# The tail of a sandwich kernel: residual added from the PSUM banks, and down products placed chunk by chunk between the steps of the routing

## The chip, the cores and the metric

The kernel runs on one core of a Trainium2 chip. The metric is the device time of one execution in microseconds. The engines are named as the profile names them: PE (matmuls, with PEld for its weight loads), DVE, ACT, POOL and SP, which only issues transfers here.

## The reference

The input x has 8 sequences of 512 rows and 256 columns, all in float32. Two blocks follow each other, each with a layernorm before and one after it:

```python
x = x + _layernorm(_L0_attn_ref(_layernorm(x), wq, bq, wkv, bkv, wo))
x = x + _layernorm(_L0_ffn_ref(_layernorm(x), gate_w, w_gate, w_up, w_down, sh_gate, sh_up, sh_down))

def _layernorm(x, axis=-1, eps=1e-05):
    m, v = mean(x), var(x)                    # over the 256 columns
    return (x - m) / sqrt(v + eps)
```

The attention has 16 heads of 128 columns in 4 groups of keys and values, is causal, and adds position codes to queries and keys. The feed-forward part has a shared expert of 352 hidden columns, `(silu(x @ sh_gate.T) * (x @ sh_up.T)) @ sh_down.T`, and 64 routed experts of 176 hidden columns. Each row chooses its 6 best experts by a softmax over 64 logits; each expert takes at most 64 rows, in the order of the rows over all 8 sequences, and the chosen outputs are added with their softmax weights.

## The kernel before

A sequence's 512 rows lie as 4 blocks of 128 (`NI`), so most tiles are 128 partitions by 4 blocks by 256 columns. The main loop runs over 128 pairs of sequence and head. In one step of it the scores of head k, the mixing of head k-2 and the output projection of head k-3 are issued. The projections of a sequence add up over its 16 heads in two PSUM banks, `po`. The feed-forward work of sequence b-1 is cut into small steps and put at fixed places of the loop over sequence b. The order of every engine's instructions is written out by hand (a manual schedule): each engine works through its own list in program order, and semaphores are placed where a tile or a bank is handed on.

The routed experts are done in two parts. The rows of sequences 0 to 4 are gathered from DRAM for all 32 pairs of experts and added back into DRAM. For sequences 5 to 7 one pair of experts ("late") still has free places; each of these sequences marks the rows for it (`marks`), gathers them by a matmul (`gather`, tile `ptx_late`), computes the pair (`gate_up`, `gate_up_hidden`, `turn_hidden`, `down`, tiles `pgu_late`, `hid_late`, `pth_late`, `ht_late`, `pd_late`, `dd_late`), and adds the result by a matmul with the turned marks `gt`. (A loop behind everything serves further pairs with free places; in the traced execution it has no round to run.) The last outputs of the early sequences come from `finish_early`, a generator whose steps read two partial sums (L661), take their statistics, scale them on ACT (L97), add x on POOL (L649) and store (L651). Sequence 4 is the last of these.

`last_part` (its head is `def last_part(before, spare)`) runs behind the last head. It has this to do: the end of sequence 6's shared expert (`shared6`), its routed result and output (`output6`); the whole feed-forward part of sequence 7; and the rest of `finish_early` (`spare`). The names that the text uses:

- `st_o`, `mv_o`, `ve_o`, `rs_o`, `shift_o`: statistics of sequence 7's attention output, taken from the banks `po`; mean and variance, variance plus epsilon, its power -1/2 (on POOL), and minus mean times that. The same with `_f` for the layernorm before the feed-forward part, and with `_y` for the one after it.
- L821 and L822: x plus the scaled attention output `o`, and the statistics of the sum. `scale_on_act` (L97) makes `o` on ACT.
- `xg`, `pt_f`, `xt2` (shown as `o_xt` by the profile, which shares its tile with `o`): the normalized rows, their transposes, and the copies of these.
- `psg`, `psu`, `gs`, `hid`: gate and up products of the shared expert for one chunk of hidden columns. There are three chunks, taken in the order 2, 1, 0. Chunk 2 is 96 wide and carries the 64 router logits in the partitions behind it; these are copied to `lg`. After the tanh (`gs`, ACT), two DVE operations (L692, L693) finish `hid` for a chunk.
- `pg`, `most`, `sc`, `top`, `left`, `chosen`, `pp`, `places`: the steps of the choices in `route`: turned logits, their maximum, exponentials (L388), the best eight, the marked choices, a running count by matmul, and each row's place with its expert.
- `py`: the down products of the shared expert (L698) together with the routed result (`dd_late` by `gt`: L714 for sequence 6, L859 for sequence 7), in two PSUM banks.

For sequence 6, chunk 2 of `hid` is ready before the last head; chunks 1 and 0 are left to `last_part`. PSUM banks come from three pools: `ps_s` (three banks, tag s), `ps_m` (three, tag m) and `ps_o` (two). A bank is given again in turn, so a matmul into it waits until the last reader of three allocations ago is done.

Of the kernel before, what the change touches and what calls it, by code (L numbers as in the profile page):

```python
# [44 lines left out]
def sandwich_kernel(ctx, tc, x, wq, bq_t, wkv, bk_t, bv, wo, gate_wt, w_gate, w_up, w_down,  # L45
# [50 lines left out]
    def scale_on_act(dst, src, rs, shift, i):  # L96
        nc.scalar.activation(dst, src, AF.Identity, bias=shift[:, i : i + 1], scale=rs[:, i : i + 1])  # L97
# [25 lines left out]
    with ExitStack() as part:  # L123
# [545 lines left out]
        def shared(b, xt2, l, banks="mmmmmm"):  # L669

            hid = p1.tile([P, len(SH_CHUNKS), T], F32, tag="hid", name=f"hid_{b}")
            banks = iter(banks)

            for n, (f0, fw) in reversed(list(enumerate(SH_CHUNKS))):
                mw = min(P, fw + NX // 2)
                pgu = []
                for w_sb, name in ((sg_sb, "psg"), (su_sb, "psu")):
                    tag = next(banks)
                    pp = {"m": ps_m, "s": ps_s}[tag].tile([P, T], F32, tag=tag, name=f"{name}_{b}_{n}")
                    for c in range(NC):  # L680
                        nc.tensor.matmul(pp[:mw, :], lhsT=w_sb[:, c, ds(f0, mw)], rhs=xt2[:, c, :],
                                         start=c == 0, stop=c == NC - 1)
                    pgu.append(pp)
                if fw < P:
                    l["lg"] = p1.tile([NX, T], F32, tag="y", name=f"lg_{b}")
                    on_act(l["lg"][: NX // 2, :], pgu[0][fw:, :])
                    on_act(l["lg"][NX // 2 :, :], pgu[1][fw:, :])

                gs = p2.tile([P, T], F32, tag="gs", name=f"gs_{b}_{n}", bufs=1)
                nc.scalar.activation(gs[:fw, :], pgu[0][:fw, :], AF.Tanh, scale=0.5)  # L690
                yield
                nc.vector.scalar_tensor_tensor(gs[:fw, :], gs[:fw, :], 1.0, pgu[0][:fw, :], ALU.add, ALU.mult)  # L692
                nc.vector.scalar_tensor_tensor(hid[:fw, n, :], gs[:fw, :], 0.5, pgu[1][:fw, :], ALU.mult, ALU.mult)  # L693
                yield
# [6 lines left out]
            if b == B - 1:  # L701
                l["py"] = [ps_o.tile([P, 2, E], F32, tag=f"o{n}", name=f"py_{b}_{n}") for n in range(2)]
                for i in range(NI):
                    products(i, l["py"][i // 2][:, i % 2, :], i % 2 == 0, False)
                yield
                return
# [14 lines left out]
        def feed_forward(b):  # L721
# [41 lines left out]
            def go(which, n=1):  # L763
                return lambda: [next(l[which]) for _ in range(n)]
# [36 lines left out]

            steps["shared"], steps["output"] = go("f"), lambda: next(l["out"]) if "out" in l else begin_output()
            return steps

        def last_part(before, spare):
# [4 lines left out]
            shared6, output6 = before["shared"], before["output"]  # L810
            shared6()
            mv, rs = norm_scales([sums[i // 2][:, i % 2, :] for i in range(NI)], f"o{b}")
            shared6()
            shared6()
            shift = shifts(mv, rs, f"o{b}")
            two = p2.tile([P, 2, NI * E], F32, tag="v", name="o_xt2")
            o, xt2 = two[:, 0].rearrange("p (i e) -> p i e", i=NI), two[:, 1].rearrange("p (c t) -> p c t", c=NC)
            st = small.tile([P, NI, 6], F32, tag="st", name=f"st_f{b}")
            for i in range(NI):
                scale_on_act(o[:, i, :], sums[i // 2][:, i % 2, :], rs, shift, i)  # L820
                nc.vector.tensor_add(xt[:, i, :], xt[:, i, :], o[:, i, :])  # L821
                nc.vector.bn_stats(st[:, i, :], xt[:, i, :])  # L822
            mv, rs = scales_of(st, NI, f"f{b}")
            shared6()
            shift = shifts(mv, rs, f"f{b}")
            nc.sync.dma_start(out=rows_of(x1_d, b * T), in_=xt)
            xg = p1.tile([P, NI, ROW], F32, tag="xg", name=f"xg_{b}")
            for i in range(NI):
                if i % 2:
                    scale_on_act(xg[:, i, :E], xt[:, i, :], rs, shift, i)  # L830
# [12 lines left out]
            next(r)  # L843
# [17 lines left out]
            shared6()  # L861
            output6()
            output6()
# [188 lines left out]
```

## Time and profile before

| what | value |
|---|---|
| median of 3 runs | 1479.51 us (1479.34 to 1482.35) |
| the profiled execution's own time | 1482.25 us |
| its span, first to last instruction | 1480.5 us |
| mean granted PE clock | 0.986 |
| busy PE, DVE, ACT, POOL | 1404.6, 887.2, 507.5, 424.8 us |
| last matmul of the last head's projection starts / `pd_late` of sequence 7 starts | 1412.30 / 1460.17 us |
| last sum (L872) ends / last store is issued | 1468.8 / 1469.33 us |

Times of single instructions count from the start of the span. A busy share says how long an engine had an instruction under way; it says nothing on whether the next one waited. For that one reads the idle time that a row gives in brackets, with what ended it. The last 70 us of the span belong to `last_part` and the wait for its stores; nothing that the change edits runs earlier.

### The profile page before, as it was taken

How to read it: one execution, taken by the hardware profiler on the slowest of the kernel's cores; microseconds unless marked ns; L12 is line 12 of the kernel's file. 1: busy time of each engine (PE TensorE's matmuls, PEld its weight loads, DVE VectorE, ACT ScalarE, POOL GpSimd, SP SyncE). 2: the span in 40 equal slices, each digit the busy share in tenths (PEclk: the TensorE clock that was granted, in tenths of full speed). 3: DMA queues.
4: the chain of work that ended last, by engine and by line, in shares of the span. 5: the costliest groups of instructions: out<-in, count | busy, mean ns of one | idle time of the engine just before them, and what ended most of it. 6: DMA issues, size and time to landing. Idle time of an engine off the chain costs nothing. (4 is left out here: it accounts for less than half of the span.)

```text
span 1480.5 us, 18545 instructions
## 1 busy us (share of the span) xinstructions
PE 1404.6 (95%) x5310; PEld 853.3 (58%) x5310; DVE 887.2 (60%) x3094; ACT 507.5 (34%) x1450; POOL 424.8 (29%) x682
## 2 busy tenths in 40 slices
PE   9999999999999999999999999989899999899985
PEld 5656655666565655665566555655455655455553
DVE  5555576657655666557665766666455554567543
ACT  2333333233422333233323333233233243344432
POOL 2222231123211321123112411234434343523311
PEclk9999999999999999999999999999999999999998
DMA  7664554355444554445435554459999889668711
GB/s 257 195 181 142 156 169 144 105 158 163 150 132 131 160 153 137 121 152 168 142 107 157 162 151 136 132 184 252 253 236 242 240 232 255 179 194 259 211 47 62
DMA packets 160790, 252.03 MB, mean 170 GB/s; under 512 B 16412, under 2 KB 136189, under 8 KB 160685
## 3 DMA queue, kind: packets, MB, share of 16 engines
q1 hardware_dynamic: 131149, 206.76, 46.4%
q10 hardware_dynamic: 23392, 34.61, 8.6%
q0 software_dynamic: 6144, 9.44, 3.4%
q8 instruction: 44, 0.72, 0.2%
q14 instruction: 61, 0.50, 0.1%
HBM read 143.01 MB, written 107.74 MB: 169 GB/s over the span
## 5 line engine op out<-in xcount | busy, mean ns | idle before, releaser
L306 POOL TENSOR_SCALAR e<-e,recip 128x128 f32<-128x128 f32 x508 | 266.2, 557 | 802.6 <-DVE recip L303 775.1
L296 ACT ACTIVATE e<-e,least 128x128 f32<-128x128 f32 (+3 forms) x512 | 285.6, 559 | 388.9 <-DVE least L293 346.0
L289 PE MATMUL psc<-kt,qt 128*128 128x128 f32 (+3 forms) x1024 | 311.2, 441 | 24.3 <-DVE least L293 12.1
L349 PE MATMUL pav<-et,v 128*128 128x512 f32 (+3 forms) x1024 | 297.2, 433 | 5.3 <-ACT dd L584 5.3
L349 PEld LDWEIGHTS pav<-et,v 128*128 128x128 f32 x1024 | 194.0, 190 | 168.4 <-issue 117.9
L293 DVE CUSTOM_DVE_ANT_0 e<-psc,mask 128x128 f32<-128x128 f32 (+3 forms) x512 | 231.4, 478 | 52.1 <-PE psc L289 46.6
L361 PE MATMUL po<-wo_sb,ao 128*128 128x256 f32 x1024 | 243.5, 381 | 0.7 <-ACT ao L109 0.7
L276 PE MATMUL pq<-xnt,wq_sb 128*128 128x512 f32 x512 | 241.7, 594 | 1.0 <-ACT sc L388 0.7
L361 PEld LDWEIGHTS po<-wo_sb,ao 128*128 128x128 f32 x1024 | 192.5, 190 | 68.7 <-issue 37.4
L322 DVE STREAM_TRANSPOSE eb<-e 128x128 f32<-128x128 f32 x756 | 227.3, 364 | 4.0 <-DMA ex_d<-eb 4.0
L289 PEld LDWEIGHTS psc<-kt,qt 128*128 128x128 f32 x1024 | 166.0, 191 | 106.4 <-DVE least L293 37.7
L109 ACT COPY ao<-pav 128x512 f32<-128x512 f32 x128 | 75.0, 586 | 436.4 <-PE pav L349 416.5
L279 DVE SCALAR_TENSOR_TENSOR qt<-pq,bq_sb,pe_sb 128x512 f32<-128x512 f32 x128 | 95.7, 748 | 110.1 <-PE pq L276 110.1
L276 PEld LDWEIGHTS pq<-xnt,wq_sb 128*128 128x128 f32 x512 | 96.3, 191 | 71.9 <-issue 64.3
L303 DVE RECIPROCAL recip<-total 128x4 f32<-128x4 f32 x128 | 22.8, 178 | 126.8 <-ACT e L296 126.8
L296 ACT ACTIVATION_READ_ACCUMULATOR e<-e,least 128x1 f32 x512 | 95.7, 187 | 0.0
L585 POOL DMA_INDIRECT y_d<-dd,idx x32 | 50.9, 1591 | 113.4 <-DMA y_d<-dd,idx 80.3
L248 PE MATMUL pk<-xnt,wkv_sb 128*128 128x512 f32 x128 | 60.4, 594 | 0.2 <-ACT xnt L109 0.2
L259 PE MATMUL pv<-wkv_sb,xnt 128*128 128x512 f32 x128 | 60.2, 593 | 0.0
L261 DVE TENSOR_TENSOR v<-pv,bv_sb 128x512 f32<-128x512 f32 x32 | 22.1, 691 | 61.8 <-PE pv L259 61.8
L251 DVE SCALAR_TENSOR_TENSOR kt<-pk,bk_sb,pe_sb 128x512 f32<-128x512 f32 x32 | 24.0, 750 | 48.9 <-PE pk L248 48.9
L112 DVE COPY ht<-pth 88x256 f32<-88x256 f32 x32 | 13.4, 418 | 63.5 <-PE pth L566 63.4
(193 smaller groups left out, 1121.5 us busy)
## 6 DMA issues: line engine op xcount, KB each, us to landing
ex_d<-eb SPq DMA_DIRECT2D x126, 640.0 KB
et<-ex_d SPq DMA_DIRECT2D x504, 160.0 KB
wgu<-in_w_gate ACTq DMA_DIRECT2D x32, 352.0 KB
wgu<-in_w_up ACTq DMA_DIRECT2D x32, 352.0 KB
wd<-in_w_down ACTq DMA_DIRECT2D x32, 352.0 KB
y<-y_d SPq DMA_DIRECT2D x10, 512.0 KB
x<-in_x SPq DMA_DIRECT2D x8, 512.0 KB
x_d<-x SPq DMA_DIRECT2D x8, 512.0 KB
```

The costliest lines, as they stand in the source:

```text
L109: nc.scalar.copy(dst, src)
L248: nc.tensor.matmul(pk, lhsT=wkv_sb[:, c, g, 0, :], rhs=s["xnt"][:, c, :], start=c == 0, stop=c == NC - 1)
L259: nc.tensor.matmul(pv, lhsT=s["xnt"][:, c, ts(i, P)], rhs=wkv_sb[:, c, :, 1, :], start=c == 0, stop=c == NC - 1)
L276: nc.tensor.matmul(pq, lhsT=wq_sb[h // QPG][:, c, ts(h % QPG, D)], rhs=seqs[b]["xnt"][:, c, :], start=c == 0, stop=c == NC - 1)
L279: nc.vector.scalar_tensor_tensor(qt, pq, bq_sb[:, h : h + 1], pe_sb, ALU.add, ALU.add)
L289: nc.tensor.matmul(psc[:, :w], lhsT=l["qt"][:, ts(i, P)], rhs=seqs[b]["kt"][h // QPG][:, :w], start=True, stop=True)
L293: nc.vector.tensor_tensor_reduce(out=e, in0=psc[:, :w], in1=mask[:, T - w :], scale=-1.0 / math.sqrt(D), scalar=BIG, op0=ALU.add, op1=ALU. ...
L296: nc.scalar.activation(e, e, AF.Exp, bias=l["least"][:, i : i + 1], scale=-1.0, accum_out=l["total"][:, i : i + 1])
L306: engine.tensor_scalar(e, e, recip[:, n : n + 1], 1.0, ALU.mult, ALU.mult)
L322: nc.vector.transpose(blocks.rearrange("p c j t -> p j c t"), l["e"][i][:, js[0] * P : (js[-1] + 1) * P].rearrange("p (j c t) -> p j c t", ...
L349: nc.tensor.matmul(pav[:, :, j:, :], lhsT=seqs[b]["v"][:, j, ts(g, D)], rhs=l["et"][:, :, AT[j] : AT[j] + NI - j, :], start=j == 0, stop=j ...
L361: nc.tensor.matmul(po[b][i // 2][:, i % 2, :], lhsT=ao[:, ts(i, P)], rhs=wo_sb[:, h, :], start=h == 0 and i % 2 == 0, stop=h == NH - 1, sk ...
```

## The change

`shared` no longer finishes everything in one order. For sequences 6 and 7 it hands out three pieces, and `last_part` places them: `hidden(n)` is the pair of DVE operations for chunk n of sequence 6, `part(py, n)` is the four down products of chunk n, and `late(py)` the four products of the routed result with the copies to `y` and the store. Chunk 0 of sequence 6 takes its `gs` from another pool tag (`qt`), so that two of them can be held.

In `last_part` the residual is added with one DVE operation from the bank, x + po * rs (L843 of the changed kernel). The shift that is left out there is added on POOL later (L861), since the layernorm that follows takes a row's mean off anyway. In the output the same is done with two DVE operations: subtract the mean from the bank (L901), then multiply and add (L903). Sequence 4's scaling and sums come first in `last_part`, its store comes last of all, and sequence 6's output is issued ahead of sequence 7's final products.

The order that this gives on each engine (sequence in brackets where it matters):

- PE: psg_1, psu_1, psg_0, psu_0 (6); chunk 2 of py (6); transposes pt_f; chunk 0; psg_2, psu_2 (7); chunk 1; pg; routed products (6); psg_1, psu_1 (7); pp; psg_0, psu_0 (7); gather; turned marks; pgu; chunks 2 and 1 (7); pth; chunk 0; pd; routed products (7).
- DVE: shift_y (4); statistics of po; four times L843 and statistics; shift_o; mv_f, ve_f; hidden(0); shift_f; two blocks of xg; hidden(1); copy of pt_f_1; the choices up to chosen; hidden of chunk 2 (7); places, marks; hidden of chunk 1 (7); copy gxt; hidden of chunk 0 (7); hid_late; copy ht; statistics of y (6); statistics of py (7); four L901; four L903.
- ACT: y scaling (4); tanh of chunks 1 and 0 (6); two blocks of xg; and from there as before without the scalings that DVE took over.
- POOL: x_4's four sums, rs_o, rs_f, four times L861, rs_y (6), x_6's four sums, rs_y (7).
- SP: x1 store, y_6 store, xg store, places store, output of 6, y_7 store, two halves of the output of 7, output of 4.

```diff
+            def part(py, n):
+                fw = SH_CHUNKS[n][1]
+                for i in range(NI):
+                    nc.tensor.matmul(py[i // 2][:, i % 2, :], lhsT=hid[:fw, n, ts(i, P)], rhs=sd_sb[:fw, n, :],
+                                     start=n == 2 and i % 2 == 0, stop=False, skip_group_check=True)
+
+            def late(py):
+                l["y"] = p1.tile([P, NI, E], F32, tag="y", name=f"y_{b}")
+                for i in range(NI):
+                    nc.tensor.matmul(py[i // 2][:, i % 2, :], lhsT=l["gt"][:, ts(i, P)], rhs=l["dd"], start=False,
+                                     stop=True, skip_group_check=True)
+                    if i % 2:
+                        on_act(l["y"][:, i - 1 : i + 1, :], py[i // 2])
+                nc.sync.dma_start(out=rows_of(ly_d, b * T - ET_ROWS), in_=l["y"])
...
-                gs = p2.tile([P, T], F32, tag="gs", name=f"gs_{b}_{n}", bufs=1)
+                gs = (p2.tile([P, T], F32, tag="qt", name=f"gs_{b}_{n}") if b == B - 2 and n == 0 else
+                      p2.tile([P, T], F32, tag="gs", name=f"gs_{b}_{n}", bufs=1))
                 nc.scalar.activation(gs[:fw, :], pgu[0][:fw, :], AF.Tanh, scale=0.5)
+
+                def hidden(n=n, fw=fw, gs=gs, pgu=pgu):
+                    nc.vector.scalar_tensor_tensor(gs[:fw, :], gs[:fw, :], 1.0, pgu[0][:fw, :], ALU.add, ALU.mult)
+                    nc.vector.scalar_tensor_tensor(hid[:fw, n, :], gs[:fw, :], 0.5, pgu[1][:fw, :], ALU.mult, ALU.mult)
...
         def last_part(before, spare):
...
-            shared6, output6 = before["shared"], before["output"]
+            other, shared6, output6 = before["l"], before["shared"], before["output"]
+            next(spare, None)
             shared6()
             mv, rs = norm_scales([sums[i // 2][:, i % 2, :] for i in range(NI)], f"o{b}")
-            shared6()
-            shared6()
-            shift = shifts(mv, rs, f"o{b}")
+            next(other["f"])
...
-            for i in range(NI):
-                scale_on_act(o[:, i, :], sums[i // 2][:, i % 2, :], rs, shift, i)
-                nc.vector.tensor_add(xt[:, i, :], xt[:, i, :], o[:, i, :])
+            for i in range(NI):
+                nc.vector.scalar_tensor_tensor(xt[:, i, :], sums[i // 2][:, i % 2, :], rs[:, i : i + 1], xt[:, i, :],
+                                               ALU.mult, ALU.add)
                 nc.vector.bn_stats(st[:, i, :], xt[:, i, :])
+            shift = shifts(mv, rs, f"o{b}")
+            py6 = [ps_o.tile([P, 2, E], F32, tag=f"o{n}", name=f"py_{b - 1}_{n}") for n in range(2)]
+            other["part"](py6, 2)
             mv, rs = scales_of(st, NI, f"f{b}")
-            shared6()
-            shift = shifts(mv, rs, f"f{b}")
-            nc.sync.dma_start(out=rows_of(x1_d, b * T), in_=xt)
+            other["hidden"](0)
+            fshift = shifts(mv, rs, f"f{b}")
...
+            other["hidden"](1)
             transpose_rows(xt2, xg, f"f{b}")
+            for i in range(NI):
+                nc.gpsimd.tensor_scalar(xt[:, i, :], xt[:, i, :], shift[:, i : i + 1], 1.0, ALU.add, ALU.mult)
+            nc.sync.dma_start(out=rows_of(x1_d, b * T), in_=xt)
+            other["part"](py6, 0)
             f = shared(b, xt2, l, "msmsms")
             next(f)
+            other["part"](py6, 1)
             r = route(b, xg, l)
-            for _ in spare:
-                pass
             next(r)
-            shared6()
+            other["late"](py6)
             next(r)
             next(r)
+            next(f)
+            next(f)
             next(r)
             marked = marks(table["m"], xg[:, :, E:ROW], table["places"], b, p2, "xnt")
             next(f)
             next(f)
             gather("late", [(xg, marked[0])])
             gt = turn_scores(marked[1], b, p2, "kt", 5)
-            next(f)
             gate_up("late")
             next(f)
+            py = l["py"] = [ps_o.tile([P, 2, E], F32, tag=f"o{n}", name=f"py_{b}_{n}") for n in range(2)]
+            l["part"](py, 2)
+            l["part"](py, 1)
             gate_up_hidden("late")
-            next(f)
             turn_hidden("late")
-            next(f)
+            l["part"](py, 0)
             down("late")
-            py = l["py"]
+            output6()
+            output6()
+            output6()
             for i in range(NI):
                 nc.tensor.matmul(py[i // 2][:, i % 2, :], lhsT=gt[:, ts(i, P)], rhs=pairs["late"]["dd"],
                                  start=False, stop=True, skip_group_check=True)
-            shared6()
-            output6()
-            output6()
...
-            shift = shifts(mv, rs, f"y{b}")
-            for i in range(NI):
-                scale_on_act(o[:, i, :], py[i // 2][:, i % 2, :], rs, shift, i)
-                nc.vector.tensor_add(xt[:, i, :], xt[:, i, :], o[:, i, :])
+            for i in range(NI):
+                nc.vector.tensor_scalar(o[:, i, :], py[i // 2][:, i % 2, :], mv[:, i, 0:1], None, ALU.subtract)
+            for i in range(NI):
+                nc.vector.scalar_tensor_tensor(xt[:, i, :], o[:, i, :], rs[:, i : i + 1], xt[:, i, :],
+                                               ALU.mult, ALU.add)
                 if i % 2:
                     nc.sync.dma_start(out=rows_of(out, b * T)[:, i - 1 : i + 1, :], in_=xt[:, i - 1 : i + 1, :])
-            output6()
+            for _ in spare:
+                pass
```

More of the change, by code (lines that the diff above doesn't have):

```diff
@@ L671, in shared @@
             hid = p1.tile([P, len(SH_CHUNKS), T], F32, tag="hid", name=f"hid_{b}")
-            banks = iter(banks)
+            banks, todo = iter(banks), {}
+            def part(py, n):
[11 more added lines that the diff above has]
+                nc.sync.dma_start(out=rows_of(ly_d, b * T - ET_ROWS), in_=l["y"])
+            l |= {"late": late, "part": part, "hidden": lambda n: todo.pop(n)()}
             for n, (f0, fw) in reversed(list(enumerate(SH_CHUNKS))):
@@ L687, in shared @@
                     on_act(l["lg"][NX // 2 :, :], pgu[1][fw:, :])
-                gs = p2.tile([P, T], F32, tag="gs", name=f"gs_{b}_{n}", bufs=1)
+                gs = (p2.tile([P, T], F32, tag="qt", name=f"gs_{b}_{n}") if b == B - 2 and n == 0 else
+                      p2.tile([P, T], F32, tag="gs", name=f"gs_{b}_{n}", bufs=1))
                 nc.scalar.activation(gs[:fw, :], pgu[0][:fw, :], AF.Tanh, scale=0.5)
+                def hidden(n=n, fw=fw, gs=gs, pgu=pgu):
+                    nc.vector.scalar_tensor_tensor(gs[:fw, :], gs[:fw, :], 1.0, pgu[0][:fw, :], ALU.add, ALU.mult)
+                    nc.vector.scalar_tensor_tensor(hid[:fw, n, :], gs[:fw, :], 0.5, pgu[1][:fw, :], ALU.mult, ALU.mult)
+                todo[n] = hidden
                 yield
-                nc.vector.scalar_tensor_tensor(gs[:fw, :], gs[:fw, :], 1.0, pgu[0][:fw, :], ALU.add, ALU.mult)
-                nc.vector.scalar_tensor_tensor(hid[:fw, n, :], gs[:fw, :], 0.5, pgu[1][:fw, :], ALU.mult, ALU.mult)
-                yield
+                if b != B - 2 or n == 2:
+                    todo.pop(n)()
+                    yield
+            if b >= B - 2:
+                return
             def products(i, py, first, last):
@@ L699, in products @@
                                      stop=last and n == len(SH_CHUNKS) - 1, skip_group_check=True)
-            if b == B - 1:
-                l["py"] = [ps_o.tile([P, 2, E], F32, tag=f"o{n}", name=f"py_{b}_{n}") for n in range(2)]
-                for i in range(NI):
-                    products(i, l["py"][i // 2][:, i % 2, :], i % 2 == 0, False)
-                yield
-                return
             y = l["y"] = p1.tile([P, NI, E], F32, tag="y", name=f"y_{b}")
@@ L800, in feed_forward @@
                                 "14B": go("out"), "15A": go("out")}
+            steps["l"] = l
             steps["shared"], steps["output"] = go("f"), lambda: next(l["out"]) if "out" in l else begin_output()
@@ L829, in last_part @@
                 if i % 2:
-                    scale_on_act(xg[:, i, :E], xt[:, i, :], rs, shift, i)
+                    scale_on_act(xg[:, i, :E], xt[:, i, :], rs, fshift, i)
                 else:
                     normalize(xg[:, i, :E], xt[:, i, :], mv, rs, i)
+            other["hidden"](1)
             transpose_rows(xt2, xg, f"f{b}")
+            for i in range(NI):
+                nc.gpsimd.tensor_scalar(xt[:, i, :], xt[:, i, :], shift[:, i : i + 1], 1.0, ALU.add, ALU.mult)
+            nc.sync.dma_start(out=rows_of(x1_d, b * T), in_=xt)
+            other["part"](py6, 0)
             f = shared(b, xt2, l, "msmsms")
             next(f)
+            other["part"](py6, 1)
             r = route(b, xg, l)
-            for _ in spare:
-                pass
             next(r)
-            shared6()
+            other["late"](py6)
             next(r)
             next(r)
+            next(f)
+            next(f)
             next(r)
```

## The prediction

> **What bounds the kernel now.** I read the page first, then the table of windows over the last 80 us, then the order of time from 1405 us on, then the groups by form for single durations. The page says that TensorE has work to the very end (its chain of waits names only the last residual sum, L872):
>
> ```profile
> PE 1404.6 (95%) x5310; PEld 853.3 (58%) x5310; DVE 887.2 (60%) x3094; ACT 507.5 (34%) x1450; POOL 424.8 (29%) x682
> ...
> PEclk9999999999999999999999999999999999999998
> ```
>
> The 95% is an average over 128 heads. The change touches only what comes after the last head, so its own stretch decides. In the windows (columns: PE, PEld, DVE, ACT, POOL busy us, granted clock, DMA share, GB/s) one row stands out:
>
> ```profile
> 1410.00:1420.00 10.00, 9.27 (x29) 5.24 (x28) 3.42 (x12) 1.70 (x4) 1.01 (x1) 1.00 0.00 0
> 1420.00:1430.00 10.00, 4.94 (x14) 2.48 (x13) 6.31 (x20) 3.58 (x8) 1.01 (x1) 0.78 0.16 55
> 1430.00:1440.00 10.00, 9.33 (x34) 6.07 (x33) 1.94 (x9) 5.47 (x16) 2.77 (x4) 0.88 0.05 16
> 1440.00:1450.00 10.00, 9.65 (x61) 6.47 (x59) 6.72 (x23) 1.77 (x3) 0.00 (x0) 1.00 0.50 167
> ```
>
> From 1421 us PE is idle for 5 us, and afterwards its clock is low. The order of time shows the chain (start, duration, engine, line, what; idle time before it and what ended that):
>
> ```profile
> 1415.66 1.01 POOL L87 TENSOR_TENSOR rs_o<-ve_o,mhalf 128x4 f32<-128x4 f32 x1 [10.58 <-DVE ve_o L85]
> ...
> 1419.97 1.93 ACT L97 ACTIVATE o_xt<-po,shift_o,rs_o 128x256 f32<-128x256 f32 x4
> ...
> 1420.57 0.43 DVE L821 TENSOR_TENSOR x<-x,o_xt 128x256 f32<-128x256 f32 x1 [2.04 <-ACT o_xt L97]
> ...
> 1426.22 2.04 PE L119 MATMUL pt_f<-ident,xg 128*128 128x128 f32 x8 [5.06 <-DVE xg L106]
> ...
> 1428.08 3.78 PE L681 MATMUL psg<-o_xt,sg_sb 128*128 128x512 f32 x4
> ...
> 1435.08 2.06 ACT L97 ACTIVATE y<-y,shift_y,rs_y 128x256 f32<-128x256 f32 x4
> ...
> 1437.05 0.30 ACT L388 ACTIVATE sc<-pg,most 128x64 f32<-128x64 f32 x1
> ...
> 1460.17 1.08 PE L575 MATMUL pd_late<-wd_late,ht_late 88*64 88x256 f32 x8
> ```
>
> The reader is to see three losses. rs_o is ready at 1416.67, but the first sum starts at 1420.57, because shift_o (1418.37) stands behind two shared-expert operations on DVE and the scaling behind a tanh on ACT. PE then waits 5.06 us, and psg takes 3.78 us where the same four matmuls take 1.88 at 1414.13. And the exponentials of the choices (L388), wanted from 1435.54 on, wait for the y scaling of an early sequence until 1437.05. From the gate transposes (1434.62) to pd (1460.17) PE is nearly full: there the order of work sets the end.
>
> **The change part by part.** All PE work is kept: 24 products py by hid, 8 by gt. PE durations at full clock, from starts in the order of time: a pair psg and psu 3.44 us (1414.13 to 1417.56), one chunk of four products 1.72 (1436.85 to 1438.15 is six passes in 1.30, a chunk is eight).
>
> 1. *x_4 moved forward.* shift, scaling and sums of sequence 4 go to the start. ACT scales right after its ao copy (end 1412.25); from first scaling to last sum took 1435.08 to 1438.57, 3.49 us, so POOL is done at 1415.75, and only then takes rs_o, which is behind it in POOL's queue. The row says nothing worse than 0.1 us against 1415.66. But ve_o (1415.41) now falls beside a POOL sum:
>
> ```profile
> L85 DVE TENSOR_SCALAR ve_o<-mv_o 128x4 f32<-128x4 f32 x8 | 3.8, 470 | 0.3
> ...
> L85 DVE TENSOR_SCALAR ve_f<-mv_f 128x4 f32<-128x4 f32 x8 | 1.4, 178 | 0.3
> ```
>
>    The same operation averages 470 ns where POOL works beside it and 178 where it does not. The Trainium skill, page "SBUF — State Buffer", section "Who interferes with whom", says why: VectorE in a two-port mode and GpSimd lock one another out for a whole instruction. By the row ve_o ends 0.3 us late on average; by the rule it waits for the running sum, to 1415.75, and ends at 1415.95. I take the rule's: rs_o 1416.0 to 1417.05. The sum by the row alone would be 0.1 us better.
> 2. *Residual straight from the banks.* No scaling on ACT, no o. Four L843 (scale, add, 128x256 from PSUM) alternate with the statistics. No such operation is in the trace; the nearest is L418 (PSUM plus SBUF, 128x256, mean 410 ns) against L821, which it replaces, 412: the four pairs keep 3.24 us (1420.57 to 1423.81). Bounds: 0 and +0.4 us (0.1 each). So 1417.1 to 1420.35, then shift_o 0.15, and 1.86 as before (1423.81 to 1425.67) to xg: 1422.4, 3.3 earlier. hidden(0) lies in that stretch now as then, beside POOL's rs_f; its tanh ends at 1420.08 as before, psu at 1421.16, neither late.
> 3. *Chunk 2 before the transposes.* It fills PE from 1421.0 to 1422.7. xg's last row block comes 1.21 after the first (1425.67 to 1426.88), at 1423.6, the transposes end at 1424.3. PE idles in crumbs only, so the clock stays full.
> 4. *hidden(1), then pt_f_1's copy on DVE*: 0.73 of xg, 1.5 of hidden, 0.69 of copy: done at 1425.4. The cover is chunk 0 on PE, 1424.3 to 1426.0; without it the wait would be 0.4. psg_2 starts at 1426.0 (before 1428.08). The four POOL sums of shift_o and x1's store move behind xg; nobody waits for them before the last sum. POOL's first may hold the second xg by one operation (502 ns by L306's form), but ACT's fourth block is later anyway: 0 to 0.3, I take 0.
> 5. *Chunk 1 before pg.* psg_2, psu_2 3.44, chunk 1 1.72: pg at 1431.2 (before 1434.62). Its input lg would be there at 1430.3, so this chunk costs 0.9 here and pays later.
> 6. *Choices.* pg to most 0.50, most 0.42, and no scaling ahead on ACT: sc at 1432.15 instead of 1437.05. To chosen's end 4.64 as before (1437.05 to 1441.69): 1436.8. Meanwhile PE does pg 0.46, the gt products 1.72, psg_1 and psu_1 3.44: to 1436.8. ly_d's store goes ahead of lxg_d's on SP, its input is older. y_6's copies on ACT follow the exponentials, as before.
> 7. *hidden(2) between chosen and places* on DVE: 1.5 us on the way to the marks (places 1438.3, before 1442.65; marks for the gather 1.82 later, 1440.1). PE does pp (0.55) and, once hidden(2)'s first half has freed the bank at 1437.55, psg_0 and psu_0, to 1441.05. So the gather starts on PE's account, at 1441.1 (before 1446.41), and hidden(2) costs 0.2.
> 8. *To pd.* Gather to pgu 2.56, pgu 1.33, both as before: 1445.0. Chunks 2 and 1: 3.44; the late hidden (ready 1446.2) is covered by them. pth 0.4, chunk 0 1.72 covering the ht copy: pd at 1450.55, 9.6 before 1460.17.
> 9. *The end.* py from dd, statistics, ve: 4.67 after pd's start as before, 1455.2. y_6's scale is ready only 3.15 after ht's copy (1455.06 to 1458.2 before), at 1452.4, so its POOL sums run to 1455.9 and, by the lock of part 1, hold ve to 1456.05 (0 to 0.7). Then rs 1.05 beside four L901; L901 is new, taken at L418's 0.43 each, 1.7, then four L903 at L872's 0.43: 1459.55, against 1468.83: 9.3 earlier. ACT's copies of y_7 end by 1455.9 and hold nothing.
> 10. *Stores.* x_4's 0.5 MB leaves last, at 1460.05, where x_6's left at 1469.33 before; x_6's goes at 1455.9. Four half-megabyte stores instead of three fall into the end: at the 338 GB/s of 1470 to 1472 they need 6.2 us from about 1456.8: 1463.0; before, the last landed near 1472.2. 9.2 earlier.
>
> Sum: 9.2 us. Of the 9.6 to pd, 3.4 come by pg, 1.5 more by sc, and the rest because sequence 6's hid products now fill PE's early wait and the four psg and psu products of chunks 1 and 0 the wait for the choices, instead of standing behind both. Unknown costs (items 1, 2, 4, 9) lie within -0.5 and +1.2. Against its own time (span 1480.5, time 1482.25, 1.75 outside the span) that is a span of 1471.3 and a time of 1473.0; the median of the runs, 1479.51, is 2.74 below the profiled time, so I expect 1479.5 - 9.2 = 1470.3, rounded up to 1470.5 for small waits not seen.
>
> **The rivals.**
> - *The clock falls all the same.* A wait of 5.06 us preceded the low clock here, and 3.43 us at 1385 (psc 3.91 us for eight, 2.42 otherwise); 1.22 us at 1364 did not. If chunk 2 comes late, psg_2 and psu_2 again cost 2.2 more: 7.0 us gain, 1472.5. Against: chunk 2 needs the banks read by 1420.0, one us before PE asks.
> - *PE's order gives part back.* Chunks ahead of pg, pth and pd hold critical work whenever a producer is early, and DVE's new hiddens hold places. If three such places cost 1 to 1.5 us each, the gain is 5 to 6: 1474. For: item 5 shows one of 0.9.
> - *Slower: the clock stays low.* The Trainium skill, page "TensorE: Matmul & The Clock Gate", section "A second HAM failure mode: psum-queue depth-cycling", has a kernel whose short PE waits between groups made the clock swing. Here the new part is full of such crumbs (0.2 before the transposes, at pp, at pgu). After 1421 some 31 us of PE work lie on the path, each at half clock costs as much again; slower than before from 9.2 us of that work at half clock, with all of it some 22 us slower (1501). By the row, 0: the stretch 1400 to 1420 has waits of 0.73 us and less, and a clock of 1.00. I take the row.
> - *No effect* would need another end than this part; the last things in the trace are this part's own sums and stores, so it gets next to nothing.
>
> **How the numbers follow.** My forecast 0.80 (1468.5 to 1472), the clock rival 0.07, PE's order 0.08, no effect 0.02, slower 0.03. The range, 1468.0 to 1474.5, takes in the first three but for the outer tenth. A measurement of this kernel can tell 0.2%, 3 us, from no change; the first three all exceed that, a fraction of the third aside: faster 0.94, same 0.03, slower 0.03.
>
> **What would show it.** Right: no PE wait over 1 us after the last po; clock 1.00 in 1420 to 1440; psg_2 in 1.9 us; L843 near 1417; sc near 1432; pd near 1450.5; last store near 1460. Wrong: ve_o or rs_o later than 1417.5, L843 above 0.55 us, a granted clock below 0.95 there, pd after 1453, or stores landing more than 3.5 us after the last issue.

## The result, and the profile after

Eight runs of the changed kernel have a median of 1469.33 us (1466.1 to 1477.28); eight of the kernel before, 1480.72 (1471.45 to 1484.6). The ratio is 0.9944, with a 95% interval of 0.992 to 0.9968: a gain of 8.3 us, between 4.7 and 11.8. (The ratio is not the quotient of the two medians, which lie 11.4 us apart; that too is inside the interval.) The forecast was 1470.5.

The profiled execution of after has a span of 1469.4 us, a time of 1471.22 and a mean clock of 0.992. Of the page:

```profile
PE 1398.0 (95%) x5310; PEld 851.9 (58%) x5310; DVE 887.6 (60%) x3097; ACT 503.8 (34%) x1442; POOL 428.9 (29%) x686
...
PEclk9999999999999999999999999999999999999998
```

The number of matmuls is the same, and their busy time is 6.6 us less, part of it time at a low clock that is gone. The share still says 95%, as before; this view would have shown nothing. The windows of after (columns as in the prediction) do:

```profile
1410.00:1420.00 10.00, 9.43 (x28) 5.31 (x29) 6.71 (x25) 3.69 (x7) 4.65 (x6) 1.00 0.01 2
1420.00:1430.00 10.00, 9.95 (x43) 6.62 (x42) 3.36 (x8) 3.43 (x6) 2.10 (x5) 1.00 0.15 53
1430.00:1440.00 10.00, 9.90 (x46) 5.58 (x45) 8.15 (x30) 2.86 (x11) 0.00 (x0) 1.00 0.38 131
1440.00:1450.00 10.00, 9.66 (x57) 7.04 (x55) 4.57 (x16) 1.71 (x4) 0.60 (x1) 1.00 0.01 2
```

From 1420 to 1430 PE was busy for 4.94 us at a clock of 0.78; it is busy for 9.95 us at 1.00. In the order of time of after:

```profile
1411.10 2.79 POOL L649 TENSOR_TENSOR x<-x,y 128x256 f32<-128x256 f32 x4 [7.90 <-ACT y L97]
...
1413.68 0.23 DVE L85 TENSOR_SCALAR ve_o<-mv_o 128x4 f32<-128x4 f32 x1
1413.99 1.02 POOL L87 TENSOR_TENSOR rs_o<-ve_o,mhalf 128x4 f32<-128x4 f32 x1
...
1415.04 0.48 DVE L843 SCALAR_TENSOR_TENSOR x<-po,rs_o,x 128x256 f32<-128x256 f32 x1 [1.13 <-POOL rs_o L87]
...
1421.01 1.48 PE L119 MATMUL pt_f<-ident,xg 128*128 128x128 f32 x8
...
1424.05 1.88 PE L699 MATMUL psg<-o_xt,sg_sb 128*128 128x512 f32 x4
...
1430.25 0.31 ACT L388 ACTIVATE sc<-pg,most 128x64 f32<-128x64 f32 x1 [1.38 <-DVE most L384]
...
1448.66 1.08 PE L575 MATMUL pd_late<-wd_late,ht_late 88*64 88x256 f32 x8
...
1453.33 0.17 DVE L85 TENSOR_SCALAR ve_y<-mv_y 128x4 f32<-128x4 f32 x1
1453.41 1.65 DVE L901 TENSOR_SCALAR o_xt<-py,mv_y 128x256 f32<-128x256 f32 x4
1454.11 1.02 POOL L87 TENSOR_TENSOR rs_y<-ve_y,mhalf 128x4 f32<-128x4 f32 x1
...
1455.16 1.67 DVE L903 SCALAR_TENSOR_TENSOR x<-o_xt,rs_y,x 128x256 f32<-128x256 f32 x4
```

pt_f follows the py products with no wait in its bracket, where before there were 5.06 us, and takes 1.48 us instead of 2.04; psg takes 1.88 instead of 3.78.

One care in reading these times. The main loop, which nobody edited, does not take the same time in two executions: the last head's projection (the last L361 on PE) starts at 1412.30 us in the trace of before, at 1410.57 in that of after, and between 1407.30 and 1417.08 in the experiments' traces. So everything below is counted from that start, the mark. What is left between two kernels is then their tail alone. The whole-run ratio, which has the loop's scatter in it, is given beside it.

| from the start of the last projection, us | before | after | difference | predicted |
|---|---|---|---|---|
| first sum of the residual starts | 8.27 | 4.47 | -3.80 | 4.8 |
| transposes pt_f start | 13.92 | 10.44 | -3.48 | about 10.5 |
| psg_2 starts | 15.78 | 13.48 | -2.30 | 13.7 |
| pg starts | 22.32 | 18.73 | -3.59 | 18.9 |
| sc starts | 24.75 | 19.68 | -5.07 | 19.85 |
| pd_late starts | 47.87 | 38.09 | -9.78 | 38.25 |
| last sum of the output ends | 56.53 | 46.26 | -10.27 | 47.25 |
| span ends | 68.20 | 58.83 | -9.37 | 59.0 |

The predicted column is the prediction's time less 1412.30. The two profiled spans differ by 11.1 us; 9.4 of them are the tail, the other 1.7 are the loop's scatter.

How PE spent the time from the mark to pd_late, before and after (columns as in the prediction):

```profile
1412.30:1460.17 47.87, 41.23 (x160) 25.53 (x160) 22.92 (x78) 12.85 (x30) 5.80 (x7) 0.93 0.15 50
1410.57:1448.66 38.09, 37.85 (x160) 24.07 (x161) 22.24 (x71) 10.90 (x26) 6.75 (x10) 1.00 0.15 49
```

The same 160 matmuls lie in both stretches. Of the 9.78 us between them, 6.40 are idle time of PE that is gone (6.64 before, 0.24 after), and 3.38 are matmuls that take less time, most of it the low clock (2.3 us by e1_fill below). Up to pd_late the new kernel has nothing left to fill.

### The profile page after: what moved, and what is told of

It reads as the page before. It is cut to its first block, busy times and chain, and to the rows that moved or that the text cites. A ratio compares the mean times of both kernels' runs of the same rounds, so it can differ in the third digit from the quotient of the medians.

```text
span 1469.4 us, 18542 instructions
## 1 busy us (share of the span) xinstructions
PE 1398.0 (95%) x5310; PEld 851.9 (58%) x5310; DVE 887.6 (60%) x3097; ACT 503.8 (34%) x1442; POOL 428.9 (29%) x686
## 5 line engine op out<-in xcount | busy, mean ns | idle before, releaser
L289 PE MATMUL psc<-kt,qt 128*128 128x128 f32 (+3 forms) x1024 | 310.6, 441 | 23.1 <-DVE least L293 11.2
L361 PE MATMUL po<-wo_sb,ao 128*128 128x256 f32 x1024 | 243.5, 381 | 0.7 <-ACT ao L109 0.7
L361 PEld LDWEIGHTS po<-wo_sb,ao 128*128 128x128 f32 x1024 | 192.6, 190 | 69.0 <-issue 37.6
L279 DVE SCALAR_TENSOR_TENSOR qt<-pq,bq_sb,pe_sb 128x512 f32<-128x512 f32 x128 | 95.8, 748 | 111.2 <-PE pq L276 111.1
```

The lines of the kernel that those rows point to most:

```text
L279: nc.vector.scalar_tensor_tensor(qt, pq, bq_sb[:, h : h + 1], pe_sb, ALU.add, ALU.add)
L289: nc.tensor.matmul(psc[:, :w], lhsT=l["qt"][:, ts(i, P)], rhs=seqs[b]["kt"][h // QPG][:, :w], start=True, stop=True)
L361: nc.tensor.matmul(po[b][i // 2][:, i % 2, :], lhsT=ao[:, ts(i, P)], rhs=wo_sb[:, h, :], start=h == 0 and i % 2 == 0, stop=h == NH - 1, sk ...
```

## The experiments

The theory, as the prediction has it: the wait of PE for `xg` cost its own 5 us and a low clock behind it; the change takes the wait away by an earlier first sum and fills what is left with sequence 6's products; with those gone from their old places the end moves as far as PE's order lets it. The rivals: the early sum does it all; the order of the products does it all; ACT's queue is to blame and not the way of the addition; the stores eat the gain. Times are again from the mark. The ratios of e1 to e4 and of e5 to e8 were taken on two chips, each against runs of before on the same chip.

| kernel | built on | PE waits before pt_f | pg | sc | pd_late | span ends | ratio to before (95%) |
|---|---|---|---|---|---|---|---|
| before | | 5.06 | 22.32 | 24.75 | 47.87 | 68.20 | 1 |
| after | | none | 18.73 | 19.68 | 38.09 | 58.83 | 0.9944 (0.992 to 0.9968) |
| e1_fill | before | none | 20.01 | 22.44 | 45.56 | 65.99 | 0.9981 (0.9964 to 0.9998) |
| e2_bank | before | 3.17 | 19.81 | 22.24 | 45.36 | 65.72 | 1.0003 (0.9982 to 1.0024) |
| e3_x4 | before | 5.06 | 20.78 | 21.74 | 46.33 | 66.63 | 0.9994 (0.9976 to 1.0012) |
| e4_behind | after | 1.57 | 16.51 | 17.47 | 40.76 | 61.52 | 0.9952 (0.9938 to 0.9966) |
| e5_store | after | none | 18.72 | 19.68 | 38.08 | 57.45 | 0.9947 (0.9928 to 0.9966) |
| e6_act_behind | after | 3.13 | 24.55 | 25.51 | 43.92 | 64.67 | 0.9974 (0.9955 to 0.9993) |
| e7_act_ahead | after | 0.31 | 19.20 | 20.15 | 38.56 | 59.41 | 0.9936 (0.9917 to 0.9955) |
| e8_order | after | none | 17.85 | 18.81 | 36.06 | 55.30 | 0.9918 (0.9894 to 0.9943) |

The intervals of the whole runs are some 4 to 7 us wide. They separate the large steps (e8 from e6, after from before), not steps of one or two, nor e8, e7 and e5 from after; for these the tail's marks, one profiled execution each, are the measurement.

**Is it the idle time that makes the clock fall?** `e1_fill` keeps before's order and lets PE do 12 products of 256 columns into an unused bank while it waits, whose result nobody reads (the profile counts two matmuls for each).

```diff
             shared6()
+            fill = ps_s.tile([P, T], F32, tag="s", name="fill")
+            for n in range(12):
+                nc.tensor.matmul(fill[:, :E], lhsT=ident, rhs=sd_sb[:, 0, :], start=True, stop=True)
```

> The kernel before, with twelve filler matmuls (128x256, result not used) behind psu of chunk 0 of sequence 6, in the stretch in which PE waits 5.06 us for the transposes. Times are counted from the start of the last projection (the last L361 on PE): before, pd_late starts 47.87 us after it. Theory A (the low clock behind that wait comes from the wait itself): psg of sequence 7's chunk 2 takes 1.9 us instead of 3.78, psu 1.9 instead of 2.29, pd_late 2.2 us earlier, at 45.7, and the span 2.2 shorter. Theory B (the low clock belongs to the place or to the transposes, not to the idle time): psg stays near 3.8 and pd_late near 47.9.

The order of time of e1_fill:

```profile
1417.21 5.34 PE L817 MATMUL fill<-sd_sb,ident 128*128 128x256 f32 x24
...
1422.39 1.52 PE L119 MATMUL pt_f<-ident,xg 128*128 128x128 f32 x8
...
1424.15 1.98 PE L681 MATMUL psg<-o_xt,sg_sb 128*128 128x512 f32 x4 [0.24 <-ACT o_xt L109]
...
1425.97 1.88 PE L681 MATMUL psu<-o_xt,su_sb 128*128 128x512 f32 x4
```

pt_f starts where it did (13.88 after the mark, 13.92 before), so nothing came earlier; yet psg and psu run at full speed (1.98 and 1.88 us) and pd_late is 2.31 us earlier. Work that nobody needs makes the kernel faster: the fall of the clock is the wait's doing, and it cost 2.3 us in these two executions. The whole runs agree, 2.8 us with an interval from 0.3 to 5.3.

**What does the addition from the banks do alone?** `e2_bank` has only that, in before's order.

```diff
-                scale_on_act(o[:, i, :], sums[i // 2][:, i % 2, :], rs, shift, i)
-                nc.vector.tensor_add(xt[:, i, :], xt[:, i, :], o[:, i, :])
+                nc.vector.scalar_tensor_tensor(xt[:, i, :], sums[i // 2][:, i % 2, :], rs[:, i : i + 1], xt[:, i, :],
+                                               ALU.mult, ALU.add)
...
+            oshift = shift
...
-            nc.sync.dma_start(out=rows_of(x1_d, b * T), in_=xt)
...
+            for i in range(NI):
+                nc.gpsimd.tensor_scalar(xt[:, i, :], xt[:, i, :], oshift[:, i : i + 1], 1.0, ALU.add, ALU.mult)
+            nc.sync.dma_start(out=rows_of(x1_d, b * T), in_=xt)
```

> The kernel before, with the first residual alone changed: x + po * rs on DVE from the banks, the shift added on POOL behind xg, x1 stored there. shift_o still stands behind chunk 1's hidden operations. Theory A (bank operation costs what L843 measured, 475 ns against 412): first sum 2.0 us earlier, pairs 0.25 us longer in all, xg 1.75 earlier, PE's wait 3.3 instead of 5.06 us. If a wait of 3.3 us still lets the clock fall, pd_late at 46.1 us after the start of the last projection; if not, 43.9. Rival: the residual is worth nothing alone because PE's order sets the end: 47.9.

```profile
1429.11 1.48 PE L119 MATMUL pt_f<-ident,xg 128*128 128x128 f32 x8 [3.17 <-DVE xg L106]
...
1430.82 3.38 PE L681 MATMUL psg<-o_xt,sg_sb 128*128 128x512 f32 x4 [0.24 <-ACT o_xt L109]
...
1433.99 2.23 PE L681 MATMUL psu<-o_xt,su_sb 128*128 128x512 f32 x4
```

The first sum comes 2.1 us earlier and the wait shrinks by 1.9, to 3.17. The transposes then still run at full speed, but psg takes 3.38 us: the clock fell all the same, late. pd_late is 2.51 us earlier, at 45.36, between the 46.1 and the 43.9 that were expected with and without a fall. In the whole runs, 12 of them, no gain is to be seen (1.0003, 0.9982 to 1.0024); the interval only just reaches a gain of 2.5 us (0.9982 is 2.7). How much of the trace's 2.51 is usual is not settled here.

**Does clearing ACT's queue for the choices pay?** `e3_x4` moves only sequence 4's scaling and sums to the front of the part.

```diff
+            next(spare, None)
             shared6()
```

> The kernel before, with sequence 4's scaling and sums alone moved to the start of the tail; its store stays where it was. sc no longer waits on ACT. Theory A (in the old order PE is full with sequence 6's sixteen products between pg and pp, so an earlier choice finds PE busy): sc 1.5 us earlier, but pd_late only 0 to 0.2 earlier, at 47.7 to 47.9 us after the start of the last projection. Rival, the step as the prediction credited it: all of the 1.5 us reach pd_late, 46.4.

```profile
1425.49 2.04 PE L119 MATMUL pt_f<-ident,xg 128*128 128x128 f32 x8 [5.06 <-DVE xg L106]
...
1427.34 2.62 PE L681 MATMUL psg<-o_xt,sg_sb 128*128 128x512 f32 x4
...
1433.31 0.31 ACT L388 ACTIVATE sc<-pg,most 128x64 f32<-128x64 f32 x1 [0.39 <-DVE most L384]
```

pd_late is 1.54 us earlier, and at first sight that is the rival's number: sc comes 0.96 us after pg instead of 2.43, and 1.47 is what was to be had. But the time from pg to pd_late is 25.55 us in both kernels (22.32 to 47.87, 20.78 to 46.33). The earlier sc reached nothing: PE was full with sequence 6's products until pp. All of the 1.54 lies ahead of pg, where psg took 2.62 instead of 3.78 after the same wait of 5.06 us: in this execution the clock came back earlier (more on that below). Two marks, not one, were needed to see it. In the whole runs, nothing (0.9994).

**What does the order of the products bring?** `e4_behind` is after with all three chunks of sequence 6 put behind pg, where before had them.

```diff
-            other["part"](py6, 2)
...
-            other["part"](py6, 0)
...
-            other["part"](py6, 1)
             r = route(b, xg, l)
             next(r)
+            for n in (2, 0, 1):
+                other["part"](py6, n)
             other["late"](py6)
```

> The changed kernel, with the three chunks of sequence 6's down products put behind pg, all in one, ahead of the routed products. Nothing else differs. Changed kernel: pd_late 38.09 us after the start of the last projection. Theory A (PE's order is what the chunks are worth, clock not touched): psg of chunk 2 at 0.85 earlier, pg and choices 1.85 earlier, but PE reaches pp 3.2 us later, so pd_late at 41.3. Rival B (without chunks 2 and 0 PE waits 1.6 us, does transposes for 1.3, and waits 0.9 again; if the clock falls in that, psg and psu cost 2 us more): pd_late at 43.3 and a granted clock below 0.95 there.

```profile
1426.11 1.47 PE L119 MATMUL pt_f<-ident,xg 128*128 128x128 f32 x8 [1.57 <-DVE xg L106]
1427.82 1.98 PE L699 MATMUL psg<-o_xt,sg_sb 128*128 128x512 f32 x4 [0.24 <-ACT o_xt L109]
...
1432.58 5.45 PE L678 MATMUL py<-sd_sb,hid 96*128 96x256 f32 x24
...
1437.53 0.29 DVE L406 TENSOR_SCALAR chosen<-left 128x256 bf16<-128x256 f32 x1
...
1443.03 0.19 PE L414 MATMUL pp<-chosen,upto 128*128 128x64 bf16 x1
```

and the window with the wait:

```profile
1420.00:1430.00 10.00, 8.14 (x24) 3.63 (x23) 7.83 (x22) 2.46 (x6) 3.05 (x6) 1.00 0.11 39
```

pg is 2.2 us earlier than in after, since nothing stands ahead of it, and pd_late is 2.67 later: chosen ends at 1437.82 us and pp starts at 1443.03, 5.2 us behind it, because PE still has other work. So the place of sequence 6's chunks is by itself worth 2.7 us at pd_late. (The new places of sequence 7's chunks and of its psg and psu have no run of their own.) A wait of 1.57 us, transposes and another 0.24 us left the clock at 1.00.

**Is it the bank operation, or its place?** `e6_act_behind` gives after the old way of adding, with the scaling on ACT behind the two tanh; `e7_act_ahead` puts the four scalings ahead of the second tanh. Both leave out POOL's later shift.

```diff
             mv, rs = norm_scales([sums[i // 2][:, i % 2, :] for i in range(NI)], f"o{b}")
-            next(other["f"])
+            oshift = shifts(mv, rs, f"o{b}")
...
             for i in range(NI):
-                nc.vector.scalar_tensor_tensor(xt[:, i, :], sums[i // 2][:, i % 2, :], rs[:, i : i + 1], xt[:, i, :],
-                                               ALU.mult, ALU.add)
+                scale_on_act(o[:, i, :], sums[i // 2][:, i % 2, :], rs, oshift, i)
+            next(other["f"])
+            for i in range(NI):
+                nc.vector.tensor_add(xt[:, i, :], xt[:, i, :], o[:, i, :])
                 nc.vector.bn_stats(st[:, i, :], xt[:, i, :])
```

(This is e7_act_ahead; e6_act_behind has `next(other["f"])` where after has it, and scaling and addition in one loop.)

> The changed kernel, with the first residual as before it: scaled on ACT into o, added on DVE, the scaling behind the tanh of sequence 6's chunk 0; no POOL sums for the shift. Everything else as in the changed kernel. Theory A (the gain of the bank operation is that it passes ACT's queue, where the tanh waits for psg): first sum at 8.2 us after the start of the last projection instead of 4.47, xg 3.5 later, PE waits some 3.5 us in front of the transposes, pd_late at 41.6 with the clock kept and 42.3 to 43.9 with a fall. Rival B (PE's order alone is what the change is worth, the wait is filled elsewhere): pd_late within 1 us of 38.1.

> As the kernel with the scaling on ACT behind the tanh, but with the scaling issued ahead of that tanh (behind the tanh of chunk 1, shift_o first on DVE). Theory A (the queue place is the whole of it; the operation saved is worth the 0.7 us of shift and first scaling, less the 0.25 us that four bank operations cost more): first sum at 5.2 us after the start of the last projection, pd_late at 38.4 to 38.6. Rival B (adding from the bank is worth more by itself): pd_late at 40 or later.

Of e6_act_behind, two windows and the order of time:

```profile
1420.00:1430.00 10.00, 6.87 (x24) 4.67 (x23) 7.53 (x21) 3.90 (x8) 1.01 (x1) 0.76 0.15 53
1430.00:1440.00 10.00, 10.00 (x35) 6.62 (x34) 0.89 (x4) 3.61 (x13) 0.00 (x0) 0.90 0.00 0
```

```profile
1420.30 1.92 ACT L97 ACTIVATE o_xt<-po,shift_o,rs_o 128x256 f32<-128x256 f32 x4
...
1426.55 2.04 PE L119 MATMUL pt_f<-ident,xg 128*128 128x128 f32 x8 [3.13 <-DVE xg L106]
...
1428.38 3.62 PE L678 MATMUL py<-sd_sb,hid 128*128 128x256 f32 x8
```

With the scaling behind the tanh, pt_f is 3.48 us later than in after, the wait is back, and the clock falls: eight py products take 3.62 us instead of 1.89. pd_late is 5.83 us later, 3.48 for the sum and 2.35 for the clock. In e7_act_ahead ACT scales at once:

```profile
1414.19 1.02 POOL L87 TENSOR_TENSOR rs_o<-ve_o,mhalf 128x4 f32<-128x4 f32 x1
...
1415.44 1.93 ACT L97 ACTIVATE o_xt<-po,shift_o,rs_o 128x256 f32<-128x256 f32 x4 [0.31 <-DVE shift_o L93]
1416.04 0.43 DVE L846 TENSOR_TENSOR x<-x,o_xt 128x256 f32<-128x256 f32 x1 [0.63 <-ACT o_xt L97]
```

pd_late is 0.47 us later than in after, and no more. So the new operation itself is worth half a microsecond; the rest of what the bank addition brings is that it need not stand in ACT's queue, and the old operation gets that too when it is issued in time. The whole runs of e7_act_ahead and after can't be told apart.

**Do the stores set the end?** `e5_store` issues sequence 4's store, last in after, right behind that of x1.

```diff
             nc.sync.dma_start(out=rows_of(x1_d, b * T), in_=xt)
+            for _ in spare:
+                pass
...
-            for _ in spare:
-                pass
```

> The changed kernel, with sequence 4's output stored right behind x1's store instead of last of all. Times count from the start of the last projection; changed kernel: pd_late at 38.09, last sum ends at 46.26, end of span at 58.83. Theory A (the end waits for 2 MB of stores that fill the transfer engines at 340 GB/s from 44.5 on; one half megabyte less is 1.5 us less): sums unmoved, end at 57.2 to 57.4. Rival B (the end follows the last issue by a fixed time, as the prediction's first count had it): the last issue is 0.9 us earlier, end at 57.9. Rival C (the transfers don't set the end): 58.8.

In slices of 0.5 us from 1450, the traffic of after:

```profile
GB/s 0 0 0 0 0 0 0 33 0 16 252 346 344 340 348 342 334 338 338 334 344 352 180 18 16 0 0 16 0 0 0 0 0 0 0 0 0 0 0 0
```

and in slices of 0.55 us from 1440, that of e5_store:

```profile
GB/s 0 0 0 0 0 0 0 30 0 0 0 0 0 0 0 0 0 0 0 0 0 30 0 0 60 339 331 354 348 343 333 348 346 73 15 15 0 15 0 0
```

In after the traffic holds near 340 GB/s for some six microseconds, while the last sum ends at 1456.83. In e5_store the sums end at the same 46.2 us, the stretch is a quarter shorter, as one store of four is gone from it, and the span ends 1.38 us earlier, at 57.45, next to theory A's 57.2 to 57.4. So the stores' traffic and not the last sum sets the end of after. Nor does the end follow the last issue by a fixed time: from the start of the last issue to the end of the span there are 11.7 us in after, 11.2 in e5_store and 10.1 in e8_order below. From the end of the traffic to the end of the span there are 8.1, 8.3 and 7.8 us (8.4 in before). In these 8 us no engine has an instruction under way and hardly a byte is moved; what they are spent on, the traces do not show.

**A version that goes on from there.** `e8_order` takes e5_store's store, puts only half of chunk 1 of sequence 6 ahead of pg (`part` takes the row blocks as a third argument), starts sequence 6's output ahead of `down`, and moves sequence 7's chunks back by one place: chunk 2 stands ahead of pth, chunk 1 ahead of `down` and chunk 0 behind it.

```diff
-            other["part"](py6, 1)
+            other["part"](py6, 1, (0, 1))
             next(r)
+            other["part"](py6, 1, (2, 3))
...
             l["part"](py, 2)
-            l["part"](py, 1)
             gate_up_hidden("late")
             turn_hidden("late")
-            l["part"](py, 0)
-            down("late")
+            l["part"](py, 1)
             output6()
+            down("late")
             output6()
+            l["part"](py, 0)
             output6()
```

> The changed kernel with what its own trace suggests: sequence 4's store early; half of sequence 6's chunk 1 behind pg instead of ahead of it (PE then waits for neither lg nor chosen, 0.65 us less); pth behind chunk 2 and pd_late behind chunk 1 of sequence 7, chunk 0 last (covers the wait for dd, 0.7 us less); sequence 6's statistics and sums from the time at which ht is copied, so that POOL is free for the last rs and x_6's store leaves earlier. If PE's order sets the end up to the last matmul and the stores behind it: last sum ends at 44.9 us after the start of the last projection instead of 46.26, end at 55.5 to 56.2 instead of 58.83, and the time 2.6 to 3.3 us below the changed kernel's. If the stores alone matter: sums at 46.2, end at 57.2.

```profile
1425.15 0.46 PE L382 MATMUL pg<-ident,lg 64*128 64x64 f32 x4
1425.54 1.13 PE L678 MATMUL py<-sd_sb,hid 128*128 128x256 f32 x4
...
1443.36 1.08 PE L575 MATMUL pd_late<-wd_late,ht_late 88*64 88x256 f32 x8
1444.37 2.00 PE L678 MATMUL py<-sd_sb,hid 128*128 128x256 f32 x8
```

pg is 0.88 us earlier than in after, pd_late 2.03, the last sum 1.03 (chunk 0 now lies between), the end 3.53, with the first of the four last stores 2 us earlier too. Not all of it went as expected. pp still starts only at 24.37 (24.41 in after), 0.9 us after chosen's end: PE stays the bound of that stretch, and the earlier pg reached nothing. Of the 2.03 us at pd_late, 1.7 are chunk 0, which now stands behind it. The last sum came at 45.23 where 44.9 was expected, and the end at 55.30, a little better than the 55.5 to 56.2. Of the 3.53 us at the end, e5_store shows 1.38 for the store alone; the rest is not split among the other edits. Six runs have a median of 1464.85 us, 0.9918 of before: the lowest ratio of the kernels here, though its interval overlaps that of after.

## Why the prediction was right, step by step

**The sum.** Predicted 9.2 us, measured 9.37 at the end of the tail, 8.3 (4.7 to 11.8) in the whole runs. Its time of 1470.5 is 1.2 above the median of after, and the 1479.51 that it started from, a median of three runs, is 1.2 below the median of all eight.

**Item 1, x_4 and the lock.** The mechanism was right and nearly without price. POOL's four sums ended at 1413.89, 0.13 us sooner than predicted. ve_o started 0.21 us before that, took 0.23 us, its lone duration being 0.17, and so ended 0.02 us behind the last sum. Before's trace shows the lock more plainly than the mean of 470 ns that the prediction read:

```profile
188.59 1.25 POOL L306 TENSOR_SCALAR e<-e,recip 128x384 f32<-128x384 f32 x2
189.30 0.57 DVE L85 TENSOR_SCALAR ve_o<-mv_o 128x4 f32<-128x4 f32 x1
```

Six of the eight ve_o in it take 0.57 to 0.58 us, and each ends 0.03 us behind POOL's operation; the other two, with POOL idle, take 0.17. So 470 is a mean of two kinds, and the prediction did well to take the rule of the Trainium skill's page "SBUF — State Buffer", section "Who interferes with whom", by which DVE waits for the whole of POOL's instruction. The trace agrees with it. What the rule added to the path was 0.06 us here, not 0.37, since the sum was nearly done, and the prediction had let ve_o take another 0.2 us after the release.

**Item 2, four sums from the banks.** Each takes 472 ns on average, not L418's 410: the four pairs lasted 3.49 us (1415.04 to 1418.53) instead of 3.24. A cost of 0.25, inside the bound of 0 to 0.4; the zero that was taken was too low. The prediction says that no such operation is in the trace; L279 has the same form, with twice the columns: a tensor in PSUM, one number per partition, a tensor in SBUF. It takes 748 ns where L692, which has a constant in place of that number, takes 687. These 61 ns on top of 410 would have come to 471. Items 1 and 2 cancel.

**Items 3 to 5.** Right: no wait ahead of pt_f, clock 1.00, psg_2 0.2 earlier than stated, chunk 1 ahead of pg. e8_order shows the cost that item 5 puts on chunk 1: half of it moved away brings pg 0.88 us.

**Items 6 to 8.** The times hold to 0.2 us. But the working that gives "1.5 more by sc" was wrong as a sum of parts: e3_x4 shows that sc's 1.5 us alone reach nothing, and e4_behind that the place of sequence 6's chunks is worth 2.7. The one pays only with the other, since PE has to be free when the choices are ready. PE's own account, 6.40 us less idle and 3.38 less busy up to pd_late, adds up where the sum by marks does not.

**Item 9, the end.** Here is the largest miss, 1 us in favour, and part of it is luck. POOL's sums for sequence 6 ended at 1454.14, where the prediction had them (43.6 after the mark). It held ve for them, by the lock. But the lock lasts one instruction and not four: ve_y starts at 1453.33, beside the third sum, and ends at 1453.50, 0.04 us behind that sum's end. The four L901 run beside the fourth sum and after it, in 1.65 us; only rs_y waits, 0.6 us, in POOL's own queue behind the fourth sum, and L901 covers that. The prediction had ve at 42.9 after the mark, just at the start of the fourth sum, and it came at 42.76. Had it come some 0.1 us later, the lock would, by the same reading, have held it to the end of that sum, 0.7 us.

**Item 10, the stores.** Right in kind, and it takes back most of item 9's gain: the last sum came 1 us sooner than predicted, the end only 0.17. e5_store shows what sets it.

**The rivals.** The clock did not fall, and PE's order gave nothing back that the sum did not have. The slower rival, from the Trainium skill's page "TensorE: Matmul & The Clock Gate", section "A second HAM failure mode: psum-queue depth-cycling", does not show: PE's micro-waits in after (up to 0.57 us in sum in each of the four windows) left the clock at 1.00 from 1410 to 1450.

**What stays open.** The clock's share of the gain is a draw. After the same wait of 5.06 us, the stretch from psg_2 to pg lasted 6.54 us in before's trace and 5.01 in e3_x4's; at full clock, in e1_fill, it is 4.37. So the low clock cost 2.17 us there in the one execution and 0.64 in the other. Here is the low clock of before, and then that of e3_x4:

```profile
1425.70:1432.40 6.70, 6.18 (x13) 3.25 (x14) 1.46 (x5) 2.18 (x4) 0.00 (x0) 0.50 0.03 9
1432.50:1440.00 7.50, 6.83 (x31) 5.11 (x30) 1.94 (x9) 4.89 (x15) 2.77 (x4) 1.00 0.06 21
```

```profile
1425.30:1428.60 3.30, 3.11 (x10) 2.14 (x11) 1.06 (x3) 1.43 (x3) 0.00 (x0) 0.50 0.42 146
1428.70:1440.00 11.30, 10.63 (x52) 7.58 (x50) 3.46 (x20) 3.66 (x13) 0.00 (x0) 1.00 0.16 58
```

By the mean clock of slices of 0.1 us, it was low from 1425.65 to 1432.48 in before, 6.83 us, and from 1425.26 to 1428.67 in e3_x4, 3.41 us: twice and once the same length. It lasted 3.41 us in e2_bank and 6.83 in e6_act_behind. All thirteen changes of the clock in before's trace, from 541.60 to 1466.61, lie on one grid of 3.413 us, to within the reading; those at 1384.69, 1388.10, 1425.65 and 1432.48 are 1, 11 and 2 steps apart. The same page, section "What's actually happening", says that the clock follows a free-running window of 3.4 us, and the trace agrees. So a low stretch lasts whole windows, and how a wait lies against the grid has a part in the cost. In before the wait of PE went on for 0.57 us past the fall, in e3_x4 for 0.23; whether that decides between one window and two is not shown, as no run moved it on purpose. So the tails' difference of 9.37 us may be some 1.5 us off the usual gain; the whole-run interval holds both.

## What to carry to other kernels

When an engine waits late in a kernel, look for work that it owes anyway and whose inputs are there, and put that into the wait; then ask what stood behind that work at its old place, because a faster producer pays only if its consumer's engine is free. When an operation is replaced by another, try the old one earlier in its queue first: here the place was worth 5.4 us, 2.35 of them the clock's, and the operation half of one. Count the marks of a tail from the last event that both kernels share, and look at two marks before a difference gets a cause.

## What was not expected of the hardware

- Waits of 3.13 us (e6_act_behind) and 3.17 us (e2_bank) let the granted clock fall, 1.57 us (e4_behind) did not. In e6_act_behind it fell at 1425.23, only 1.8 us after PE's last product had ended, and the transposes were slow at once (2.04 us). In e2_bank the transposes ran in 1.48 us, and the fall came at 1431.27, 2.2 us after they had started. The length of a wait alone does not say when the clock falls.
- A scale and add of 128x256 takes 472 ns with one operand in PSUM (L843) and 479 with both in SBUF (L903), where the plain addition of PSUM and SBUF takes 410. The difference goes with the scale that is read per partition: L438, of the same form but with a constant, takes 390.
- Four L901 took 471 to 475 ns each, with a POOL sum running beside the first two or not: no sign of contention for an operation that reads PSUM.
- The issue of a store on SP, 0.36 to 0.46 us otherwise, can take longer while transfers run. In after the two halves of the last output took 0.38 and 0.81 us (377 and 806 ns in the first row below) and sequence 4's store 0.70; in e8_order the store of y_7 took 1.60 (last row) and the two behind it 0.38 each. What holds an issue back is not shown.

```profile
L906 SPq DMA_DIRECT2D out_dram<-x x2: 377/592/806, 1456.1 to 1456.9; - x2
1457.72 0.70 SPq L651 DMA_DIRECT2D out_dram<-x  x1
1449.54 1.60 SPq L902 DMA_DIRECT2D ly_d<-y  x1
```
